# A gated feed-forward block on one core: the fourth of seven products for two tiles, and where lookup steps stand

## The chip, the cores and the metric

One core of one Trainium2 chip. The time is the device time of one execution in microseconds, the median over runs of the whole kernel. All matmuls are in float32.

## The reference

Eight sequences of 1024 rows and 512 columns. Each row is normalized; a small attention with decays gives `s`; a feed-forward block, whose three weight matrices are looked up in a table of 16 values, gives `g`; the result is `x + s * silu(g)`.

```python
def _ghost_linear(x, idx, lut):
    w = lut[idx]
    return jnp.einsum('bsh,oh->bso', x, w)
gate = _ghost_linear(x, gate_idx, lut)      # idx: 1376 x 512
up = _ghost_linear(x, up_idx, lut)          # idx: 1376 x 512
h = silu(gate) * up
g = silu(_ghost_linear(h, down_idx, lut))   # idx: 512 x 1376
x = x + s * g
```

## The kernel before

**Two phases.** Phase 1 (to about 584 us) goes over the eight sequences (batches) in chunks of 128 rows: normalization, transposition, projections, attention. In between, VectorE looks up the weights: `look_up` makes, for a piece of 128 x 1024 indices, three tests of a bit, a shift, eight leaves (L224) and seven predicated copies (L241), one instruction a step. GpSimd makes sums of the looked-up blocks, and DMAs write them to HBM: `quad_d` holds the weights of pairs of tiles with all seven combinations, `wgu_d` the plain seven products of a single tile. `phase_1` places the steps by hand: three places in each chunk, with so many steps in each (`steps`). DMAs that must wait are put off by a count of ticks (`defer`).

Phase 2 (from 584 us) takes the batches one by one. The 1376 hidden columns are eleven tiles of 128 (the last has 96). Gate and up are made together as one product of 2 x 2 blocks by a scheme with seven products instead of eight (`W_OF`, `X_OF` number them). For the quads of tiles (`quads`, two of four tiles each) each of these seven products is in turn made by seven smaller ones, in a `Node`: products 1, 5, 6, 2, 7, 3, 4 of 128 x 256, into four PSUM banks (s11, s12, s21, sE), with copies on ScalarE and additions on VectorE in PSUM between them. `Node.sixth` adds to bank s12 (L920), `Node.seventh` adds s21 into sE (L924), and product (2, 4), the fourth smaller product, accumulates into s21 after that. Two nodes are woven: while one is at its sixth and seventh, the first and fifth product of the following one are issued.

Tiles 8 and 9 are a pair. Their nodes serve two of the outer seven products each: (1, 6), (5, 7), (2, 3). The outer product 4 stands alone, and class `Fourth` makes it plainly: for each of the two tiles two matmuls of 128 x 512, as two banks' worth, from the plain weights in `wgu_d`. It fills the place of the following node after (2, 3).

The eleventh tile is made by `single`, with seven products of 96 x 512 (L845): before the quads for the first batch, after them for the seven others. Inside it `at_last(5)` lets VectorE make five sums of h for the down stage (L1122). Then `down` makes the third matrix's product from h, in nodes of its own kind (L1154, L1165).

In the first batch, the lookup of the last two rows of down weights (`left_weights`) still runs during the quads: `some(made, n)` makes n steps at each node.

`x` blocks in SBUF are overwritten with sums at one place each; `restore` fetches the plain block again by a DMA on ScalarE's queue, when the plain products need it. Weight tiles go through a ring of three slots (tag "wr"), loaded by SP's queue.

**Order.** `keep_order` fixes on every compute engine the order in which the code issues instructions. Each engine is in order, so an instruction that waits holds all behind it.

Of the kernel before, what the change touches and what calls it, by code (L numbers as in the profile page):

```python
# [9 lines left out]
F32 = mybir.dt.float32  # L10
# [4 lines left out]
ALU = mybir.AluOpType  # L15
AX = mybir.AxisListType

P = 128
# [30 lines left out]
def recurrent_block(ctx: ExitStack, tc, x, wq, wk, wv, wo, wg, decay_logits, out_scale, lut, gidx, uidx, didx, out):  # L49
# [196 lines left out]
    def ffn_weights(build, pool, pair_pool):  # L246
# [10 lines left out]
        def gate_up(o):  # L257
            s, m = OCH[o]
            n = 2 * NV * m
            idx = build.tile([P, NB], I32, name="idx", tag="idx", bufs=2)  # L260
            iv = idx[:, :n].rearrange("p (a b) -> p a b", b=m)
            gs, us = (src[:, s : s + m].rearrange("(c p) b -> p c b", p=P) for src in (gidx, uidx))
            nc.sync.dma_start(out=iv[:, 2:6, :], in_=gs)
            nc.sync.dma_start(out=iv[:, 0:2, :], in_=us[:, 0:2, :])
            nc.sync.dma_start(out=iv[:, 6:8, :], in_=us[:, 2:4, :])
            yield
            wf = pool.tile([P, 2 * NB], F32, name="wgu", tag="wgu", bufs=3)
            yield from look_up(build, wf[:, :n], idx[:, :n], P, n)
            w = wf[:, : 2 * n].rearrange("p (k two m) -> p k two m", two=2, m=m)
            a21, a11, a12, a22, s1, s2, s3, s4 = (w[:, k] for k in range(8))  # L270
            nc.gpsimd.tensor_tensor(s1, a21, a22, ALU.add)
            nc.gpsimd.tensor_tensor(s2, s1, a11, ALU.subtract)
            yield
            nc.gpsimd.tensor_tensor(s3, a11, a21, ALU.subtract)
            nc.gpsimd.tensor_tensor(s4, a12, s2, ALU.subtract)
            wide = wf[:, 2 * m : 2 * n].rearrange("p (a b) -> p a b", b=m)
            if o >= 4 * NQ:
                defer(3, lambda: nc.sync.dma_start(out=wgu_d[o], in_=wide))
            if o >= 2 * NK:
                return  # L280
            if o % 2 == 0:
                upper.append(w[:, 1:])
                return
            up, low = upper.pop(), w[:, 1:]
            to = quad_d[o // 4][:, :, o // 2 % 2, :].rearrange("p k (t m) -> p k t m", m=P)
            pair = pair_pool.tile([P, 7, 3, P], F32, name="pair", tag="pair")
            nc.sync.dma_start(out=to[:, :, 0:2, :], in_=up)
            b21, b22, b11, b12 = low[:, :, 0], low[:, :, 1], up[:, :, 0], up[:, :, 1]
            nc.gpsimd.tensor_tensor(pair[:, :, 0], b21, b22, ALU.add)
            yield  # L290
            nc.gpsimd.tensor_tensor(pair[:, :, 1], pair[:, :, 0], b11, ALU.subtract)
            yield
            if o >= 4 * NQ:
                for _ in range(4):
                    yield
            nc.gpsimd.tensor_tensor(b21, b11, b21, ALU.subtract)
            defer(3, lambda: nc.sync.dma_start(out=to[:, :, 2:4, :], in_=low))
            yield
            nc.gpsimd.tensor_tensor(pair[:, :, 2], b12, pair[:, :, 1], ALU.subtract)
            defer(4, lambda: nc.sync.dma_start(out=to[:, :, 4:7, :], in_=pair))  # L300
            for _ in range(3):
                yield
# [398 lines left out]
    def phase_1():  # L701
        nonlocal small, p_a, p_c, p_r
        with (
# [37 lines left out]
            for b in range(B + 1):  # L741
                following = project(b + 1, pools, sides, kept) if b + 1 < B else iter(())
                older = chunks(b - 1, (chk, blp), kept) if b else iter(())
                for k in range(NC):


                    if b == 0:
                        steps = (k > 0, k >= NC // 2, 2 * (k >= NC // 2))
                    elif b < B:
                        steps = ((1, 1, 4), (1, 2, 4), (1, 2, 4), (1, 2, 3))[k % 4]  # L750
                    else:
                        steps = (1, 0, 0)
                    tick()
# [40 lines left out]
    def phase_2():  # L794
        with (
# [32 lines left out]
                    nc.gpsimd.tensor_tensor(o, x1, x2, ALU.subtract)  # L828
                    yield

            def single(b, o, xs, h_tail, at_last, room):

                s, m = OCH[o]
                w = ring.tile([P, 14, P], F32, name=f"wr{b}_{o}", tag="wr")
# [8 lines left out]
                def product(ps, k, start, stop):  # L843
                    for n in range(2):
# [6 lines left out]
                            skip_group_check=True,  # L851
                        )

                product(pa, 1, True, False)
                nc.scalar.copy(u2, pa)
                product(pb, 6, True, True)
                nc.vector.tensor_tensor(u2, pb, u2, ALU.add)
                at_last(5)
                nc.scalar.copy(pc, u2)
                product(pe, 5, True, False)  # L860
                nc.scalar.copy(e, pe)
                product(pa, 2, False, True)
                nc.scalar.activation(sg, pa, AF.Silu)
                product(pc, 7, False, False)
# [9 lines left out]
            class Node:  # L874
# [2 lines left out]

                def __init__(self, b, q, ks, xs):  # L880
                    self.ks, self.xs = ks, xs

                    self.restores = ks if q == NQ else (4,) if (q, ks) == (NQ - 1, (4, 4)) else ()
                    name = f"{b}_{q}_{ks[0]}"
                    self.w = ring.tile([P, 2, 7, P], F32, name=f"wq{name}", tag="wr")
                    w = self.w.rearrange("p a t m -> p a (t m)")
# [2 lines left out]
                    else:  # L889
                        for a, k in enumerate(ks):  # L890
                            nc.sync.dma_start(out=w[:, a, :], in_=quad_d[q][:, W_OF[k], 0, :])
                    self.t = [bank(r, f"{r}{name}") for r in ("s11", "s12", "s21", "sE")]
                    self.name = f"e{name}"

                def product(self, n, i, start=False):
                    for a in range(2):
                        nc.tensor.matmul(  # L897
                            self.t[n][:, ts(a, H)],
                            lhsT=self.w[:, a, (0, 1, 6, 3, 4, 5, 2)[i - 1], :],
# [9 lines left out]

                def fifth(self):  # L910
                    self.product(3, 5, True)
                    self.e = tmp.tile([P, U], F32, name=self.name, tag="e")

                def fifth_copy(self):
                    nc.scalar.copy(self.e, self.t[3])  # L915
# [7 lines left out]
                    self.product(2, 7)  # L923
                    nc.vector.tensor_tensor(self.t[3], self.t[2], self.e, ALU.add)  # L924

            class Fourth:


                def __init__(self, b, xs, u3):
                    self.b, self.xs, self.u3 = b, xs, u3  # L930
                    self.w = ring.tile([P, 14, P], F32, name=f"w4{b}", tag="wr")
                    for r in range(2):
                        nc.sync.dma_start(
                            out=self.w[:, ts(r, 2), :], in_=wgu_d[4 * NQ + r][:, ts(W_OF[4], 2), :]
                        )

                def product(self, r, role):
                    ps = bank(role, f"{role}{self.b}_4_{r}")
                    for n in range(2):
                        nc.tensor.matmul(  # L940
                            ps,
                            lhsT=self.w[:, 2 * r + n, :],
                            rhs=self.xs[:, X_OF[4], ts(n, 2), :],
                            start=n == 0,
                            stop=n == 1,
                            skip_group_check=True,
                        )
                    o = self.u3[:, ts(r, 2), :]
                    return lambda: nc.vector.tensor_tensor(o, ps.rearrange("p (a t) -> p a t", a=2), o, ALU.add)

                def first(self):
                    self.product(0, "s11")()

                def fifth(self):
                    self.add = self.product(1, "sE")

                def fifth_copy(self):
                    self.add()

            def quads(b, xs, h, sums, made, at_last):  # L960

# [53 lines left out]
                def pair_steps():  # L1017
# [2 lines left out]
                        (t[:, :, :H], t[:, :, H:])  # L1020
                        for t in (tmp.tile([P, 4, U], F32, name=f"{k}{b}_l", tag=k) for k in ("p1", "u2"))
                    )
                    room[0] = u3

                    def of_h(half, n):
                        r, c = divmod(n, 2)
                        t = half * U + c * H
# [11 lines left out]
                    def node_23(t, n):  # L1039
# [2 lines left out]
                        nc.vector.tensor_tensor(of_h(1, n), t[n][:, H:], u2[:, n], ALU.add)  # L1042
                        nc.scalar.activation(of_h(1, n), of_h(1, n), AF.Silu)

                    def after_57():
                        for n in (0, 3, 1, 2):
                            nc.gpsimd.tensor_tensor(e5[:, n], e5[:, n], u3[:, n], ALU.add)

                    def after_23():
                        for half, other in ((0, u3), (1, e5)):  # L1050
                            for n in (0, 3, 1, 2):
                                nc.gpsimd.tensor_tensor(of_h(half, n), of_h(half, n), other[:, n], ALU.mult)

                    yield (1, 6), node_16, None
                    yield (5, 7), node_57, after_57
                    yield (2, 3), node_23, after_23

                room = [None]
                def every():
                    for q in range(NQ):  # L1060
                        for ks, empty, after in steps(q):
                            yield Node(b, q, ks, xs), empty, after
                    for ks, empty, after in pair_steps():
                        yield Node(b, NQ, ks, xs), empty, after
                    yield Fourth(b, xs, room[0]), None, None
                    yield None, None, None

                todo = every()
# [4 lines left out]
                while empty:  # L1073
# [7 lines left out]
                    at_last(node.ks == (2, 3))  # L1081
                    node.seventh()
                    empty(node.t, 3)
                    some(made, 4 if node.ks in ((1, 1), (5, 5)) else 1)
                    node.product(1, 3)
                    empty(node.t, 1)
                    at_last(node.ks in ((5, 7), (2, 3)))
                    if following:
                        following.fifth()
# [281 lines left out]
            for b in range(B):  # L1371
# [24 lines left out]
                    some(more, 2)  # L1396
                    single(b, NO - 1, xs, h_tail, sums_beside, tmp)
                made = left_weights(sp, wd_left) if b == 0 else iter(())
                quads(b, xs, h, more, made, no_sums if b else at_last)
                if b == 0:  # L1400
                    hold(out=wd_tail[: OCH[-1][1], :], in_=wdt_d)
                else:
                    single(b, NO - 1, xs, h_tail, at_last, tmp2)
                nodes_done = [0]

                def beside(k):
# [59 lines left out]
```

## Time and profile before

| | |
|---|---|
| median of 3 runs | 2103.63 us (2103.54 to 2104.08) |
| the profiled execution | 2103.83 us |
| its span, first to last instruction | 2101.9 us |
| mean granted TensorE clock | 0.999 |
| TensorE busy | 2086.2 us, 99% |
| VectorE busy | 1441.4 us, 69% |
| ScalarE busy | 943.6 us, 45% |
| GpSimd busy | 1038.5 us, 49% |
| DMA from HBM and to HBM | 281.95 MB, 75.63 MB |

PE is TensorE (PEld its weight loads), DVE VectorE, ACT ScalarE, POOL GpSimd, SP the queue that issues most DMAs. A float32 matmul stands in the trace as two records, each with its own weight load. Matmul records overlap: one of 256 columns lasts 380 ns and the next begins 216 ns after it. "idle before <- X" says how long an engine stood and what released it.

### The profile page before, as it was taken

The page shows a single profiled execution, that of the slowest core. Times are in us where ns is not written, and L with a number is a line of the kernel's source. Part 1 is how long each engine was busy: PE and PEld are TensorE (multiplying, and loading weights), DVE is VectorE, ACT ScalarE, POOL GpSimd, SP SyncE. Part 2 cuts the span into 40 slices and gives each one's busy share as a digit, 9 for nine tenths or more (in the row PEclk, how much of TensorE's full clock was granted, in tenths as well). Part 3 has the DMA queues.
Part 4 walks back from the last instruction along what each step waited for, and adds up shares of the span by engine and source line. Part 5 has one row for each costly group of instructions (what it writes and reads, how often), then busy time and mean ns, then how long its engine had stood idle before and what let it go on. Part 6 is the DMA issues. An engine that isn't in the chain of part 4 may idle for free.

```text
span 2101.9 us, 32181 instructions
## 1 busy us (share of the span) xinstructions
PE 2086.2 (99%) x11691; PEld 1751.8 (83%) x11691; DVE 1441.4 (69%) x2214; ACT 943.6 (45%) x2116; POOL 1038.5 (49%) x1050
## 2 busy tenths in 40 slices
PE   9999999999999999999999999999999999999999
PEld 7887888888878888797878888787988888797877
DVE  8889998879357775675567456656755665675567
ACT  4766676676344324423531542344144224424531
POOL 4554664364364456517443741664275265527432
PEclk9999999999999999999999999999999999999999
DMA  8766769654754734554454446345544634464442
GB/s 218 147 178 165 208 149 211 158 164 125 210 177 139 258 134 161 169 216 145 157 215 152 160 151 238 138 149 196 189 146 153 249 128 158 151 233 145 146 156 106
DMA packets 184347, 359.68 MB, mean 171 GB/s; under 512 B 50895, under 2 KB 122206, under 8 KB 184190
## 3 DMA queue, kind: packets, MB, share of 16 engines
q1 hardware_dynamic: 168742, 330.61, 50.4%
q10 hardware_dynamic: 10968, 12.34, 1.8%
q0 software_dynamic: 4480, 14.68, 1.7%
q8 instruction: 93, 1.52, 0.3%
q14 instruction: 64, 0.52, 0.1%
HBM read 281.95 MB, written 75.63 MB: 170 GB/s over the span
## 4 chain that ended last, share of the span: by engine, by line
PE 81%; DVE 2%; DMA 1%; issue 0%; POOL 0%; ACT 0%; SPq 0%; DVEq 0%; ACTq 0%
PE s L897 33%; PE sE L897 6%; PE s12d L1154 5%; PE s21d L1154 5%; PE s11d L1154 5%; PE fs L845 3%; PE pd L1272 3%; PE ps L1279 3%; PE pv L444 2%; PE sEd L1154 2%; PE po L684 2%; PE fsE L845 1%; PE s11d L1165 1%; PE s12d L1165 1%; PE s21d L1165 1%; PE sEd L1165 1%
## 5 line engine op out<-in xcount | busy, mean ns | idle before, releaser
L897 PE MATMUL s<-xs,wq 128*128 128x256 f32 x3264 | 732.3, 380 | 2.3 <-DVE s L920 2.3
L897 PEld LDWEIGHTS s<-xs,wq 128*128 128x128 f32 x3264 | 620.0, 190 | 98.8 <-issue 8.4
L920 DVE TENSOR_TENSOR s<-s,e 128x512 f32<-128x512 f32 x136 | 95.1, 699 | 189.4 <-ACT s L919 189.4
L1243 POOL TENSOR_TENSOR cu<-cu 128x256 f32<-128x256 f32 x32 | 35.1, 1096 | 306.5 <-DVE cl L1242 306.5
L444 PE MATMUL pv<-wvg_sb,xnT 128*128 128x387 f32 x512 | 177.5, 488 | 0.2 <-DMA wvg_sb<-in_wv 0.2
L828 POOL TENSOR_TENSOR xs<-xs 128x256 f32<-128x256 f32 x224 | 171.8, 793 | 6.8 <-PE fs L845 2.3
L924 DVE TENSOR_TENSOR sE<-s,e 128x512 f32<-128x512 f32 x136 | 95.1, 699 | 104.0 <-PE s L897 104.0
L990 POOL TENSOR_TENSOR u<-u,e 128x512 f32<-128x512 f32 x64 | 80.4, 1278 | 134.1 <-DVE u L986 101.9
L915 ACT COPY e<-sE 128x512 f32<-128x512 f32 x136 | 79.6, 585 | 142.5 <-PE sE L897 142.5
L897 PE MATMUL sE<-xs,wq 128*128 128x256 f32 x544 | 140.5, 381 | 0.0
L444 PEld LDWEIGHTS pv<-wvg_sb,xnT 128*128 128x128 f32 x512 | 94.2, 190 | 54.1 <-issue 0.4
L994 POOL TENSOR_TENSOR h<-h,u 128x512 f32<-128x512 f32 x64 | 81.1, 1287 | 110.2 <-DVE u L1001 110.2
L423 POOL TENSOR_SCALAR rstd<-rstd 128x1 f32<-128x1 f32 x56 | 26.6, 475 | 205.9 <-ACT junk L422 204.8
L908 ACT COPY s<-s 128x512 f32<-128x512 f32 x136 | 77.5, 570 | 109.6 <-PE s L897 106.2
L919 ACT COPY s<-s 128x512 f32<-128x512 f32 x136 | 77.5, 570 | 97.8 <-PE s L897 97.8
L1154 PE MATMUL s12d<-wdd,z 128*128 128x128 f32 x896 | 118.4, 275 | 0.6 <-ACT s12d L1176 0.6
L897 PEld LDWEIGHTS sE<-xs,wq 128*128 128x128 f32 x544 | 104.0, 191 | 14.3
L1154 PEld LDWEIGHTS s12d<-wdd,z 128*128 128x128 f32 x896 | 109.0, 192 | 0.8 <-ACT s12d L1176 0.8
L224 DVE TENSOR_SCALAR leaf<-idx,lut_x,lut_sb 128x1024 int32<-128x1024 int32 (+2 forms) x119 | 108.2, 933 | 0.0
L641 POOL TENSOR_TENSOR qb<-ga,q_tab 128x384 f32<-128x384 f32 x56 | 77.1, 1377 | 55.5 <-DVE ga L637 37.8
L241 DVE COPY_PREDICATED leaf<-bit,leaf 128x1024 f32<-128x1024 uint8 (+2 forms) x68 | 93.0, 1368 | 1.7
L1283 POOL TENSOR_TENSOR gx<-gx,cu 128x512 f32<-128x512 f32 x32 | 40.8, 1278 | 82.0 <-DVE cu L1281 64.5
(266 smaller groups left out, 4517.3 us busy)
## 6 DMA issues: line engine op xcount, KB each, us to landing
wq<-quadd SPq DMA_DIRECT2D x112, 896.0 KB, 4.5
wdd<-wdd SPq DMA_DIRECT2D x56, 896.0 KB, 4.7
xs<-xsd SPq DMA_DIRECT2D x56, 512.0 KB, 6.5
wq<-quadd SPq DMA_DIRECT2D x48, 448.0 KB, 4.0
x<-in_x SPq DMA_DIRECT2D x64, 256.0 KB, 6.4
xsd<-ts SPq DMA_DIRECT2D x16, 1024.0 KB, 12.8
gx<-in_x SPq DMA_DIRECT2D x64, 256.0 KB, 6.1
out<-gx POOLq DMA_DIRECT2D x56, 256.0 KB, 2.3
```

The costliest lines, as they stand in the source:

```text
L224: nc.vector.tensor_scalar(o.bitcast(I32), iv, lut_x[:rows, k, :], lut_i[:rows, k, 0:1], ALU.bitwise_and, ALU.bitwise_xor,)
L241: nc.vector.copy_predicated(o, bits[level - 1][:rows, :n], t[:rows, :n])
L444: nc.tensor.matmul(pv, lhsT=xnT[:, v, ts(c, P)], rhs=wvg_sb[:, v, :], start=(v == 0), stop=(v == NV - 1))
L828: nc.gpsimd.tensor_tensor(o, x1, x2, ALU.subtract)
L845: nc.tensor.matmul(ps, lhsT=w[:, 2 * W_OF[k] + n, :m], rhs=xs[:, X_OF[k], 2 * n : 2 * n + 2, :], start=start and n == 0, stop=stop and n == 1,
L897: nc.tensor.matmul(self.t[n][:, ts(a, H)], lhsT=self.w[:, a, (0, 1, 6, 3, 4, 5, 2)[i - 1], :], rhs=self.xs[:, X_OF[self.ks[a]], D_OF[i], : ...
L920: nc.vector.tensor_tensor(self.t[1], self.t[1], self.e, ALU.add)
L924: nc.vector.tensor_tensor(self.t[3], self.t[2], self.e, ALU.add)
L990: nc.gpsimd.tensor_tensor(o[:, n], o[:, n], other[:, n], ALU.add)
L994: nc.gpsimd.tensor_tensor(of_h(half, n), of_h(half, n), two(other[:, n]), ALU.mult)
L1154: nc.tensor.matmul(self.t[n][:, ts(a, P)], lhsT=self.lhs[i][:, e, ts(a, P)], rhs=self.w[:, e, D_OF[i], :], start=start and a == 0 and e == ...
L1165: nc.tensor.matmul(self.t[n][:, ts(a, P)], lhsT=self.left[:, ts(2 * (n // 2) + a, P)], rhs=wd_left[:, D_OF[self.k], ts(n % 2, P)], start=F ...
```

## The change

1. In phase 1, the third place of chunks 0 and 4 of a batch makes three lookup steps instead of four.
2. The plain weights of tiles 8 and 9 are no longer written to `wgu_d`, and four empty steps that kept the pair's sums apart from that write are gone.
3. In the first batch's quads, the steps of `left_weights` at the nodes (1, 1) and (5, 5) are not four in a row but two before product (1, 3) and one or two after it.
4. `Fourth` is gone. The outer product 4 of tiles 8 and 9 is a `Node` with one entry, `(4,)`: seven products of 128 x 256, with its weights from `quad_d`. In the first batch it is the last node of the quads. In the others it is kept in `last`, and `beside_single` issues its parts between the eleventh tile's products: first and fifth before product 1; sixth and (0, 2) before 6; seventh and (1, 3) before 5; (2, 4) before 2.
5. The restore of the x block of product 4 moves from the last quad's last node to this node, and the multiplies of h by u3 wait for it.

```diff
-            if o >= 4 * NQ:
+            if o >= 2 * NK:
                 defer(3, lambda: nc.sync.dma_start(out=wgu_d[o], in_=wide))
...
-            if o >= 4 * NQ:
-                for _ in range(4):
-                    yield
...
-                        steps = ((1, 1, 4), (1, 2, 4), (1, 2, 4), (1, 2, 3))[k % 4]
+                        steps = ((1, 1, 3), (1, 2, 4), (1, 2, 4), (1, 2, 3))[k % 4]
...
+            def beside_single(node, empty, after, restore):
+                node.first()
+                node.fifth()
+                node.fifth_copy()
+                yield
+                node.sixth()
+                node.product(0, 2)
+                empty(node.t, 0)
+                yield
+                node.seventh()
+                restore(*node.restores)
+                empty(node.t, 3)
+                node.product(1, 3)
+                empty(node.t, 1)
+                yield
+                node.product(2, 4)
+                empty(node.t, 2)
+                after()
+                yield
...
+                next(beside, None)
                 product(pa, 1, True, False)
                 nc.scalar.copy(u2, pa)
+                next(beside, None)
                 product(pb, 6, True, True)
                 nc.vector.tensor_tensor(u2, pb, u2, ALU.add)
                 at_last(5)
                 nc.scalar.copy(pc, u2)
+                next(beside, None)
                 product(pe, 5, True, False)
                 nc.scalar.copy(e, pe)
+                next(beside, None)
                 product(pa, 2, False, True)
...
-            class Fourth:
...
-                    yield Fourth(b, xs, room[0]), None, None
...
+                    yield (4,), node_4l, lambda: multiply_by(0, u3)
...
+                        if ks == (4,) and b > 0:
+                            last.append((Node(b, NQ, ks, xs), empty, after, restore))
+                        else:
+                            yield Node(b, NQ, ks, xs), empty, after
...
-                    some(made, 4 if node.ks in ((1, 1), (5, 5)) else 1)
+                    some(made, 2 if node.ks in ((1, 1), (5, 5)) else 1)
                     node.product(1, 3)
                     empty(node.t, 1)
+                    some(made, (node.ks == (1, 1)) + 2 * (node.ks == (5, 5)))
...
-                    single(b, NO - 1, xs, h_tail, at_last, tmp2)
+                    single(b, NO - 1, xs, h_tail, at_last, tmp2, beside_single(*last[0]))
```

More of the change, by code (lines that the diff above doesn't have):

```diff
@@ L829, in sums_of_x, with single @@
                     yield
-            def single(b, o, xs, h_tail, at_last, room):
+            def beside_single(node, empty, after, restore):
[17 more added lines that the diff above has]
+                yield
+            def single(b, o, xs, h_tail, at_last, room, beside=iter(())):
                 s, m = OCH[o]
@@ L881, in __init__ @@
                     self.ks, self.xs = ks, xs
-                    self.restores = ks if q == NQ else (4,) if (q, ks) == (NQ - 1, (4, 4)) else ()
+                    self.restores = ks if q == NQ else ()
                     name = f"{b}_{q}_{ks[0]}"
@@ L891, in __init__ @@
                             nc.sync.dma_start(out=w[:, a, :], in_=quad_d[q][:, W_OF[k], 0, :])
-                    self.t = [bank(r, f"{r}{name}") for r in ("s11", "s12", "s21", "sE")]
+                    self.n = len(ks) * H
+                    self.t = [bank(r, f"{r}{name}")[:, : self.n] for r in ("s11", "s12", "s21", "sE")]
                     self.name = f"e{name}"
                 def product(self, n, i, start=False):
-                    for a in range(2):
+                    for a in range(len(self.ks)):
                         nc.tensor.matmul(
@@ L911, in fifth @@
                     self.product(3, 5, True)
-                    self.e = tmp.tile([P, U], F32, name=self.name, tag="e")
+                    self.e = tmp.tile([P, U], F32, name=self.name, tag="e")[:, : self.n]
                 def fifth_copy(self):
@@ L924, in seventh, with quads @@
                     nc.vector.tensor_tensor(self.t[3], self.t[2], self.e, ALU.add)
-            class Fourth:
[L929 to L960, printed above, removed]
+            def quads(b, xs, h, sums, made, at_last, last):
                 def restore(*ks):
@@ L1022, in pair_steps @@
                     )
-                    room[0] = u3
                     def of_h(half, n):
@@ L1043, in node_23, with multiply_by @@
                         nc.scalar.activation(of_h(1, n), of_h(1, n), AF.Silu)
+                    def multiply_by(half, other):
+                        for n in (0, 3, 1, 2):
+                            nc.gpsimd.tensor_tensor(of_h(half, n), of_h(half, n), other[:, n], ALU.mult)
                     def after_57():
@@ L1049, in after_23, with node_4l @@
                     def after_23():
-                        for half, other in ((0, u3), (1, e5)):
-                            for n in (0, 3, 1, 2):
-                                nc.gpsimd.tensor_tensor(of_h(half, n), of_h(half, n), other[:, n], ALU.mult)
+                        multiply_by(1, e5)
+                    def node_4l(t, n):
+                        nc.vector.tensor_tensor(u3[:, n], t[n], u3[:, n], ALU.add)
                     yield (1, 6), node_16, None
@@ L1056, in pair_steps @@
                     yield (2, 3), node_23, after_23
-                room = [None]
+                    yield (4,), node_4l, lambda: multiply_by(0, u3)
                 def every():
@@ L1063, in every @@
                     for ks, empty, after in pair_steps():
-                        yield Node(b, NQ, ks, xs), empty, after
-                    yield Fourth(b, xs, room[0]), None, None
+                        if ks == (4,) and b > 0:
+                            last.append((Node(b, NQ, ks, xs), empty, after, restore))
+                        else:
+                            yield Node(b, NQ, ks, xs), empty, after
                     yield None, None, None
@@ L1398, in phase_2 @@
                 made = left_weights(sp, wd_left) if b == 0 else iter(())
-                quads(b, xs, h, more, made, no_sums if b else at_last)
+                last = []
+                quads(b, xs, h, more, made, no_sums if b else at_last, last)
                 if b == 0:
```

## The prediction

> **What bounds the kernel now.** I read the granted clock first (0.999 over the span), then the page's engine table and chain, then the chain in order of time, then TensorE's own waits, then the timeline at the places that the change touches.
>
> ```profile
> PE 2086.2 (99%) x11691; PEld 1751.8 (83%) x11691; DVE 1441.4 (69%) x2214; ACT 943.6 (45%) x2116; POOL 1038.5 (49%) x1050
> ```
>
> TensorE is busy 99% of the span and the chain that ended last is 81% PE: what any other engine does costs nothing until TensorE waits for it. In the chain by time a node of 28 matmul records (seven products of four) follows the one before at 6.04 us (846.13, 852.18, 858.22) and one batch the one before at 188.29 us (968.73, 1157.02, 1345.31), with no wait in it. So a change is worth the TensorE records that it removes, less every new wait. TensorE's waits are few:
>
> ```profile
> PE po L684 <- DVE pr L662: 2.5, 3, 1.4
> PE s L897 <- DVE s L920: 2.3, 1, 2.3
> PE pe L505 <- DVE ts L515: 1.6, 3, 0.8
> ```
>
> The columns are total us, times, longest. The middle one lies in the first batch's nodes, where phase 2 still does a lookup:
>
> ```profile
> 644.88 3.07 DVE L224 TENSOR_SCALAR leaf<-idx,lut_x,lut_sb 128x1024 int32<-128x1024 int32 x2
> ...
> 647.99 2.26 DVE L241 COPY_PREDICATED leaf<-bit,leaf 128x1024 f32<-128x1024 uint8 x1
> ...
> 650.15 1.74 DVE L224 TENSOR_SCALAR leaf<-idx,lut_x,lut_sb 128x1024 int32<-128x1024 int32 x1
> 651.81 0.69 DVE L920 TENSOR_TENSOR s<-s,e 128x512 f32<-128x512 f32 x1
> ```
>
> Four lookup steps in a row hold back VectorE's L920, TensorE stands from 650.28 to 652.55, and then the clock halves for one window (columns: window, its length, busy us and counts, clock, DMA):
>
> ```profile
> 649.52:652.93 3.41, 1.14 (x6) 0.69 (x5) 3.41 (x4) 0.56 (x1) 1.82 (x1) 1.00 0.31 128
> 652.93:656.34 3.41, 3.41 (x10) 2.70 (x9) 2.77 (x5) 0.25 (x1) 0.00 (x0) 0.50 0.02 5
> ```
>
> Node to node the two nodes here take 9.15 (644.94 to 654.09) and 7.16 us (to 661.25) instead of 6.04: 4.2 us lost, 2.4 of it the wait (counted to where the record before stops streaming) and 1.8 the half clock.
>
> **Matmuls** (lines are those of before). `Fourth` is eight records of 512 columns, at 0.429 us each (28 of L845 take 884.80 to 896.82): 3.43 us. The seven products are 14 records of 256 columns, at 0.216 (24 take 5.18): 3.02. That is -0.41 us a batch, -3.3 in eight.
>
> **Seven batches (b > 0), first new wait.** Node (2, 3) now runs with no following node woven in. By the timeline at b = 1 its products would end: sixth 877.92, product (0, 2) 878.78, seventh 879.65, (1, 3) 880.51. Its ScalarE copy L919 ends at 878.74, just in time for the seventh. VectorE runs L920 to 879.47, then two narrow adds (0.33 us apart, from 879.38), then L924, which reads the bank that product (2, 4) writes: 880.05 to 880.74. So (2, 4) starts at 880.79: +0.27 us. `Fourth`'s 1.72 us between had hidden this.
>
> **Second new wait, the large one.** In the changed program's order VectorE has, inside the eleventh tile: the add of product 6 (L857's), five sums for the down stage (L1122, from `at_last(5)`), and only then the new node's L924-type add, which reads the bank s21 that product (2, 4) of the same node accumulates into. That product stands between the eleventh tile's products 5 and 2, and TensorE is in order, so all behind it waits. By the steps of 0.216 and 0.429 a record: (2, 4) of node (2, 3) ends 881.65, the new first and fifth 882.51, product 1 884.23, the new sixth and (0, 2) 885.09, product 6 886.81, the new seventh and (1, 3) 887.67, product 5 889.39: TensorE is there. VectorE's add of product 6 starts 0.25 us after that product, at 887.06, the sums 0.61 later, at 887.67. They take, by the timeline of before:
>
> ```profile
> 888.49 0.69 DVE L857 TENSOR_TENSOR t<-fs,t 96x512 f32<-96x512 f32 x1 [2.73 <-PE fs L845]
> 889.10 0.68 DVE L1122 TENSOR_TENSOR z<-h 128x512 f32<-128x512 f32 x1
> 889.81 1.10 DVE L1122 TENSOR_TENSOR z<-z,h 128x512 f32<-128x512 f32 x1
> 890.84 0.68 DVE L1122 TENSOR_TENSOR z<-h 128x512 f32<-128x512 f32 x1
> 891.44 0.68 DVE L1122 TENSOR_TENSOR z<-h,z 128x512 f32<-128x512 f32 x1
> 892.04 1.21 DVE L1122 TENSOR_TENSOR sx<-h 128x1024 f32<-128x1024 f32 x1
> ```
>
> Start to start 0.71, 0.61 (the 1.10 is beside a busy GpSimd; here GpSimd waits for the new node's adds), 0.60, 0.60, then 1.13 for the wide one: 3.65 us, so the new add runs 891.32 to 891.75 (0.43, L1188's row) and TensorE goes on at 891.80: +2.4 us. In before the same five sums hid because product 4, the next to need VectorE, came two products later. Bounds: 1.8, if all five follow each other at the shortest step, 0.60; 4.7, if GpSimd stretches all as it stretched that one (1.10 for 0.68). I take 2.4, because nothing of GpSimd's is due then.
>
> Per batch -0.41 + 0.27 + 2.4 = +2.3; seven, +15.8. Behind this product TensorE is the bound again; ScalarE's and VectorE's ends move along.
>
> **Transfers.** The eleventh tile's weights (L835) still go at 877.25, once node (5, 7) frees their ring slot, and land 5.0 us later (median): 882.25, while product 1 now wants them at 882.51 instead of 884.80. I count nothing and bound it by 0.3 a batch. The new node's weights are one issue on SP's queue instead of two (448 KB for 256), 10 us ahead. The restore of its x slot (128 KB, 2.0 us) moves into ScalarE's queue behind the copy L859, near 888.4; it lands near 890.4, and product 4 wants it after 897. Without that cover it would cost up to its 2.0.
>
> **The clock.** After the 2.3 us gap above, the window that held it had 1.14 us of matmul in 3.41 and the next was granted 0.50. The 1.37 us gap at 98 us, inside one window, cost nothing. A gap of 2.3 us lies inside one window, or mostly, in about half of the batches, so I take half: 7 x 0.5 x 1.8 = +6.3; bounds 0 and 12.6. The Trainium skill (TensorE: Matmul & The Clock Gate, The HAM clock gate) has the clock fall after an idle window of about 3.4 us, and speaks of gaps above that; by that rule alone no gap here would cost clock, and the sum would be 6.3 lower. The row above disagrees, with a shorter gap, and I go by it.
>
> **First batch.** The lookup steps go 2 + 1 and 2 + 2 around product (1, 3), 12 a round for 13. By counting them on, the four of 644.88 become a copy and two leaves, before the same L920. Beside GpSimd, at 2.26, 1.53 and 1.5, they end near 650.3; TensorE, ready at 650.1, goes on near 651.05. So 0.9 of the 4.2 stays: -3.3 (bounds -4.2 and -1.9). The next batch of four is two leaves and two copies (4.4 us beside an idle GpSimd), inside the node's slack of 4.6.
>
> Here the eleventh tile went first, so the new node stands alone at the end, with nothing between its products. Its copy t2 waits on ScalarE behind the last Silu of node (2, 3), which waits for VectorE's adds and sums there: about 707.6 by 700.96 + one add of 0.7, three sums (0.7, 0.7, 1.3) and nine narrower ops, while TensorE is there at 705.7. Then (1, 3) waits some 0.45 for the add behind those sums, (2, 4) some 0.3 for the next, and (2, 4) of node (2, 3) 0.3 as in the other batches: 0.3 + 1.9 + 0.45 + 0.3 - 0.41 for the matmuls = +2.5. Bounds: 1.1 (VectorE without the sum of 1.3) and 4.6 (with the clock halved and 0.3 more). The multiplies for h that the down stage's first `rest` reads come early enough: the first of them is free at about 709.6, `rest` comes 4.5 after 709.7.
>
> **Phase 1.** In seven batches the third place of chunks 0 and 4 makes 3 lookup steps instead of 4, so 14 come later; four empty steps and two writes of 896 KB go. The lookups still end about one chunk later than before, well ahead of the end of phase 1, where VectorE is less full (133.95 of 200 us in 400 to 600, 178.93 in the first 200). TensorE's waits there sum to some 5 us, so it cannot gain more; a bunching of steps behind `pr` or `ts` could lose as much as the four steps above, 4. I take 0.
>
> **Sum:** 15.8 + 6.3 - 3.3 + 2.5 = +21.3 on the profiled execution's 2103.83 us (span 2101.9 and 1.93 around it; the median of runs is 2103.63, 0.2 lower): 2125.
>
> **Rivals.**
> - The new waits cost no clock: 2103.8 + 15.0 = 2119. For it: the 1.37 us gap that cost none. Chance 0.25.
> - The clock halves in all seven batches: 2131. For it: the one gap of this length did. Chance 0.22.
> - The new node is covered, and the kernel ends no slower: VectorE would have to reach the node's add by 889.4, so the five sums would have to take 1.25 us instead of 3.65; from there on only the matmuls count (seven times -0.41, -2.9) and the first batch (-3.3 + 2.5): 2100, or 2098.7 with the lone node at its lower bound. The rows of the sums speak against it. Chance 0.06, half of it within 0.2%.
> - Phase 1's new order adds 4 us or more: 2129 to 2135. Chance 0.07.
> - My forecast, some of the gaps at half clock: 0.40.
>
> **Range.** 2112 (1.8 a wait, no clock loss, phase 1 gains 2) to 2141 (every clock lost, a third of the GpSimd stretching, phase 1 loses 4). Outside lies the covered case and some of the tails. A measurement of this kernel tells about 0.2%, 4.2 us, from no change. Faster 0.03, same 0.03, slower 0.94.
>
> **What would show it.** Right: a TensorE wait for the new node's VectorE add, seven times, about 2.3 us each; batch period near 190.6 or 192.4 us in place of 188.29; several half-clock windows; the wait at 650 under 1 us. Wrong: TensorE at 99.5% with a period of 187.9, or the eleventh tile's products waiting for a DMA.

## The result, and the profile after

The changed kernel takes 2122.2 us (median of 4 runs, 2121.65 to 2123.05) beside 2103.59 for the kernel before: a measured ratio of 1.0093, 95% interval 1.0078 to 1.0108 (1.0088 by the two medians). It is 0.9% slower. The profiled execution has a span of 2120.7 us against 2101.9.

The engine table of the page, kernel after:

```profile
PE 2090.1 (99%) x11739; PEld 1760.3 (83%) x11739; DVE 1453.2 (69%) x2246; ACT 950.2 (45%) x2140; POOL 1028.9 (49%) x1050
```

TensorE's busy time rose by 3.9 us, though by the prediction's count its matmuls need 3.3 less: a record that no neighbour overlaps counts to its full length, and one at half clock lasts longer (512 columns 1.06 us, against 0.59). The rest of the 18.8 is idle time. TensorE's own waits, kernel after (total us, times, longest):

```profile
PE s L921 <- DVE sE L948: 15.8, 8, 2.2
PE po L681 <- DVE pr L659: 1.8, 3, 1.1
PE pe L502 <- DVE ts L512: 1.5, 2, 0.8
PE s L921 <- ACT s L943: 1.4, 1, 1.4
PE psc L657 <- DVE ga L634: 1.4, 1, 1.4
```

The first line is new: product (2, 4) of the new node waits for the add of `seventh` (now L948) in all seven later batches; the eighth, of 0.35, is node (2, 3) of the first. VectorE's timeline at b = 1, kernel after:

```profile
886.51 0.69 DVE L877 TENSOR_TENSOR t<-fs,t 96x512 f32<-96x512 f32 x1 [0.88 <-PE fs L863]
887.12 0.68 DVE L1119 TENSOR_TENSOR z<-h 128x512 f32<-128x512 f32 x1
...
889.65 1.22 DVE L1119 TENSOR_TENSOR sx<-h 128x1024 f32<-128x1024 f32 x1
890.78 0.43 DVE L948 TENSOR_TENSOR sE<-s,e 128x256 f32<-128x256 f32 x1
```

and TensorE's there:

```profile
887.17 1.88 PE L863 MATMUL fsE<-xs,wr 128*96 128x512 f32 x4
891.26 0.70 PE L921 MATMUL s<-xs,wq 128*128 128x256 f32 x2 [2.21 <-DVE sE L948]
```

The five sums fill 887.12 to 890.78, 3.66 us. The last record of product 5 lasts 0.59 us, of which it streams 0.43, so TensorE stands 0.16 us longer than the row says: 2.37 us. Two small waits before it hide in the overlap of records: the 26 records up to and with the new node's first product (875.59 to 881.58) take 5.99 us instead of 5.61. In the chain by time the first full node of each of the seven later batches starts thus, kernel after (the lines between are left out):

```profile
779.84 4.40 PE s L921 x20
970.58 4.40 PE s L921 x20
1161.75 4.40 PE s L921 x20
1352.51 4.40 PE s L921 x20
1543.26 4.40 PE s L921 x20
1735.69 4.40 PE s L921 x20
1926.43 4.40 PE s L921 x20
```

A batch takes 190.74 us instead of 188.29, the second 191.17, the fifth 192.43. The second waited for the eleventh tile's weights (DMA wr, 0.43 in all), the fifth ran one window at half clock (columns: window, length, busy us and count of PE, PEld, DVE, ACT and POOL, granted clock, DMA share, GB/s; the fourth batch first, then the fifth):

```profile
1460.26:1463.67 3.41, 1.47 (x4) 0.33 (x2) 3.38 (x6) 0.82 (x2) 0.00 (x0) 1.00 0.18 56
1463.67:1467.08 3.41, 3.14 (x9) 1.46 (x10) 1.40 (x4) 0.59 (x1) 2.10 (x3) 1.00 0.44 101
1651.40:1654.82 3.42, 1.21 (x4) 0.30 (x3) 3.32 (x6) 0.58 (x1) 0.00 (x0) 1.00 0.15 45
1654.82:1658.23 3.41, 3.41 (x6) 1.47 (x7) 1.09 (x3) 0.00 (x0) 2.08 (x3) 0.50 0.42 97
```

The waits in the fourth and fifth batch are equally long; only in the fifth does the whole gap lie inside one window.

In the first batch the lookup's wait fell from 2.27 to 0.60 with no half clock behind it, and at the end TensorE waits three times, first in node (2, 3), then twice in the lone node, and the clock halves behind it (TensorE's timeline, kernel after; the first line is the lookup's wait):

```profile
650.51 1.13 PE L921 MATMUL s<-xs,wq 128*128 128x256 f32 x4 [0.60 <-DVE s L944]
...
700.34 1.99 PE L921 MATMUL s<-xs,wq 128*128 128x256 f32 x8 [0.35 <-DVE sE L948]
703.78 0.70 PE L921 MATMUL s<-xs,wq 128*128 128x256 f32 x2 [1.44 <-ACT s L943]
705.09 1.76 PE L921 MATMUL s<-xs,wq 128*128 128x256 f32 x4 [0.61 <-DVE s L944]
706.64 1.92 PE L1151 MATMUL s11d<-wdd,h 128*128 128x128 f32 x8
```

### The profile page after: what moved, and what is told of

Read it like the earlier page. It is cut to its first block, busy times and chain, and to the rows that moved or that the text cites. A ratio compares the mean times of both kernels' runs of the same rounds, so it can differ in the third digit from the quotient of the medians.

```text
span 2120.7 us, 32343 instructions
## 1 busy us (share of the span) xinstructions
PE 2090.1 (99%) x11739; PEld 1760.3 (83%) x11739; DVE 1453.2 (69%) x2246; ACT 950.2 (45%) x2140; POOL 1028.9 (49%) x1050
## 4 chain that ended last, share of the span: by engine, by line
PE 91%; DVE 5%; DMA 2%; issue 1%; ACT 0%; POOL 0%; SPq 0%; DVEq 0%; ACTq 0%; POOLq 0%
PE s L921 34%; PE pv L441 7%; PE sE L921 6%; PE s11d L1151 5%; PE s12d L1151 5%; PE s21d L1151 5%; PE fs L863 3%; PE po L681 3%; PE pd L1269 3%; PE ps L1276 3%; PE sEd L1151 2%; PE pe L502 2%; PE pc L502 2%; PE pa L502 2%; PE psc L657 2%; PE pu L667 1%
## 5 line engine op out<-in xcount | busy, mean ns | idle before, releaser
L921 PE MATMUL s<-xs,wq 128*128 128x256 f32 x3360 | 758.3, 380 | 18.5 <-DVE sE L948 15.8
L921 PEld LDWEIGHTS s<-xs,wq 128*128 128x128 f32 x3360 | 635.8, 190 | 127.6 <-DVE sE L948 25.4
L948 DVE TENSOR_TENSOR sE<-s,e 128x512 f32<-128x512 f32 x144 | 98.5, 684 | 103.3 <-PE s L921 103.3
L932 ACT COPY s<-s 128x512 f32<-128x512 f32 x144 | 80.6, 559 | 109.5 <-PE s L921 107.5
L943 ACT COPY s<-s 128x512 f32<-128x512 f32 x144 | 80.6, 560 | 97.5 <-PE s L921 97.5
L985 POOL TENSOR_TENSOR h<-h,e 128x512 f32<-128x512 f32 x64 | 81.2, 1304 | 0.0
## 6 DMA issues: line engine op xcount, KB each, us to landing
xsd<-ts SPq DMA_DIRECT2D x16, 1024.0 KB, 14.1
```

The costliest lines, as they stand in the source:

```text
L921: nc.tensor.matmul(self.t[n][:, ts(a, H)], lhsT=self.w[:, a, (0, 1, 6, 3, 4, 5, 2)[i - 1], :], rhs=self.xs[:, X_OF[self.ks[a]], D_OF[i], : ...
L985: nc.gpsimd.tensor_tensor(of_h(half, n), of_h(half, n), two(other[:, n]), ALU.mult)
```

## Experiments

The theory was that VectorE's order makes the wait (the sums ahead of the node's add), against the rival that VectorE, or something beside it, has too much to do there.

**The sums after the node's part.** In `single` of the changed kernel:

```diff
-                at_last(5)
                 nc.scalar.copy(pc, u2)
                 next(beside, None)
+                at_last(5)
```

> The changed kernel with the five sums of at_last(5) issued after the third part of the new node instead of before it; the work is the same, only VectorE's order differs. Theory (order): the wait of 2.37 us before product (2, 4), with the 0.1 that the restart costs, goes in all seven batches; a batch falls from 190.74 to about 188.3 us, the one half-clock window among them goes too, and the time is about 2103 us. Rival (VectorE has too much to do in this stage, wherever it stands): the wait moves to the next product that needs VectorE, product 4 of the eleventh tile, and a batch stays at 190 us or more, 2118 us or more.

Measured: 2103.96 us beside 2103.38 of before (ratio 1.0002, interval 0.9993 to 1.0012). Batches take 188.27, two of them 188.61 and 188.67. VectorE's timeline of this run shows the same work in another order, and in the later batches TensorE no longer waits for it:

```profile
887.00 0.69 DVE L877 TENSOR_TENSOR t<-fs,t 96x512 f32<-96x512 f32 x1 [0.89 <-PE fs L863]
887.61 0.42 DVE L948 TENSOR_TENSOR sE<-s,e 128x256 f32<-128x256 f32 x1
...
892.17 1.21 DVE L1119 TENSOR_TENSOR sx<-h 128x1024 f32<-128x1024 f32 x1
893.31 0.41 DVE L1046 TENSOR_TENSOR u_l<-s,u_l 128x256 f32<-128x256 f32 x1
```

It is the order. One line moved gives back nearly the whole loss.

**Six sums, and three.** The changed kernel with `at_last(6)` and nothing later, then with `at_last(3)` and three later.

> The changed kernel with six sums instead of five at that place (the sixth, 128x1024, taken from later in the tile). Theory: the wait grows by one step of the wide sum, 1.13 us, to 3.5 us in each of seven batches, a batch is 191.9 us without clock loss; 2.2 us of idle in one window of 3.41 us halved the clock, 1.94 did not, so with 3.3 idle most of the batches, some 5 of 7, lose another 1.7: 2122 + 7.9 + 6.8 = 2137 us. If the clock fell only after a whole window of 3.4 us idle, no batch would lose it: 2128 us. Rival (VectorE's total, not its order): a batch is unchanged, 190.7.

> The changed kernel with three sums at that place instead of five, and the other two with the one later in the tile. Theory: two steps of 0.60 and 1.13 us less in front of the new node's add, so the wait falls from 2.21 to about 0.48, a batch takes 189.0 us, no batch's clock falls; about 2108 us. Rival (the wait is not the sums'): unchanged, 190.7 a batch.

Measured with six, one run: 2142.6 us (2137 forecast), all seven waits 3.34 us. The one batch without clock loss takes 191.87, as forecast; the others 193.57 to 194.74. With three, one run: 2109.32 us (2108 forecast), waits of 0.47 us, batches of 189.30, one of 189.78, and no half clock. So the wait is the sums' time less what TensorE has beside them, step by step. The clock is dearer than forecast: in six batches of seven it halved, in four of them for two windows. In these four the rest of the gap fell into the first half-clock window; in the other two that window was full. Windows of the run with six, batches 2 and 4:

```profile
1081.18:1084.59 3.41, 1.26 (x3) 0.16 (x1) 3.38 (x6) 0.61 (x2) 0.00 (x0) 1.00 0.18 56
1084.59:1088.01 3.42, 2.23 (x4) 1.35 (x5) 2.32 (x5) 0.00 (x0) 1.67 (x3) 0.50 0.02 4
1088.01:1091.42 3.41, 3.41 (x5) 1.13 (x4) 0.00 (x0) 0.59 (x1) 0.42 (x1) 0.50 0.79 265
...
1470.30:1473.71 3.41, 1.40 (x4) 0.28 (x2) 3.38 (x6) 0.75 (x2) 0.00 (x0) 1.00 0.16 48
1473.71:1477.12 3.41, 2.08 (x6) 1.11 (x7) 2.46 (x5) 0.00 (x0) 1.53 (x3) 1.00 0.23 34
```

**The split lookup steps alone**, in the kernel before:

```diff
-                    some(made, 4 if node.ks in ((1, 1), (5, 5)) else 1)
+                    some(made, 2 if node.ks in ((1, 1), (5, 5)) else 1)
                     node.product(1, 3)
                     empty(node.t, 1)
+                    some(made, (node.ks == (1, 1)) + 2 * (node.ks == (5, 5)))
```

> The kernel before, with only the lookup steps of phase 2 set in twos around product (1, 3). Theory: the wait of 2.27 us near 650 us shrinks to 0.6 and the half clock behind it does not come; batches stay at 188.29; 2103.6 - 3.4 = about 2100.2 us. Rival (the wait comes from GpSimd's multiplies slowing VectorE, whatever the order): 2103.6, the wait unchanged.

Measured: 2100.96 us, ratio 0.999 (0.9981 to 1.0, so only just clear of no change). The wait is 0.96 us, with no half clock, batches 188.29; from the eleventh tile's first product to the second batch 191.16 us instead of 194.18, so 3.0 of the 3.4 forecast. By the trace this part of the change is worth having. VectorE's steps are still longer beside GpSimd's multiplies (a predicated copy of 128x1024 takes 2.38 us beside them and 1.31 after them), and the wait is not gone.

**The node between (5, 7) and (2, 3)**, in all batches, nothing woven into the eleventh tile:

```diff
                     yield (5, 7), node_57, after_57
+                    yield (4,), node_4l, None
                     yield (2, 3), node_23, after_23
-                    yield (4,), node_4l, lambda: multiply_by(0, u3)
```

> The changed kernel with the node of the outer product 4 woven between the nodes (5, 7) and (2, 3) in all batches, and nothing between the eleventh tile's products. Theory: no 2.4 us wait; node (2, 3) is still without a following node, so its two short waits of 0.37 us in sum stay: -0.41 + 0.37 a batch, 188.25 us; the first batch saves 3.4 at the lookup and loses about 1 at its end instead of 3.1: about 2100.5 us. Rival (the sums u3 from GpSimd come too late for this node, and VectorE waits for them with the node's other adds behind): 0.5 to 1 us more in each batch, 2104 to 2108 us.

Measured: 2106.93 us, ratio 1.0018 (1.0008 to 1.0028). Batches take 188.64 to 189.65, not the 188.25 forecast, and the cause is neither the theory's nor the rival's. TensorE's waits, this run:

```profile
PE fs L863 <- DMA xs<-xsd: 3.0, 6, 1.2
```

The restore of the x blocks of products 2 and 3 is issued at 882.92 on ScalarE's queue, and product 2 of the eleventh tile, due at 887.55, starts at 888.87. With the new node out of the way it comes earlier than the block lands. The first batch did profit: 191.72.

**Phase 1's steps alone**, in the kernel before, `(1, 1, 4)` to `(1, 1, 3)`:

> The kernel before with only phase 1's third place at three lookup steps instead of four in chunks 0 and 4. Theory (phase 1 moves nothing that TensorE waits for): phase 2's first matmul of the eleventh tile at 584 to 585 us, where three profiles with the steps of before have it at 584.0 to 585.2, and no difference that the interval can tell, 2103. Rival (the lookups ran too close to their limit, or now bunch later): 2 us or more either way.

Measured: 2109.35 us, ratio 1.0033 (1.0021 to 1.0045): the rival was right. Its TensorE has a wait that before did not have, of 5.8 us at 570 us, and two windows at half clock behind it (the kernel after has that line with 1.4, above):

```profile
PE psc L660 <- DVE ga L637: 5.8, 1, 5.8
```

SP's queue tells why (the start of each issue; this run first, then before):

```profile
555.77 0.51 SPq L343 DMA_DIRECT2D wdd<-pair  x1
556.37 0.61 SPq L468 DMA_DIRECT2D gTd<-g  x1
...
570.53 0.33 SPq L483 DMA_DIRECT2D ga<-gTd  x1
```

```profile
540.37 2.27 SPq L343 DMA_DIRECT2D wdd<-pair  x1
...
553.72 0.36 SPq L468 DMA_DIRECT2D gTd<-g  x1
...
565.05 0.33 SPq L483 DMA_DIRECT2D ga<-gTd  x1
```

The last write of down weights goes at 555.77 now, and the write of the gates, which stands behind it, directly after, at 556.37, though VectorE has the gates ready at 553.16; in before it went at 553.72. The read that must follow its landing goes at 570.53, in before at 565.05, and VectorE's product with the gates, `ga`, waits for that. Of these 5.5 us the later issue of the write is 2.65; the rest is that the write takes 14.1 us to land instead of 11.3, and why it does is not shown. In the changed kernel the last write of down weights goes at 551.09 and the read at 566.34: with four empty steps dropped, the lookups are four steps further on. The two edits belong together; that these four steps, and not the two missing writes, make up for the loss is argued from the code and was not tried alone.

**Versions without these waits.** Sums after the node's part; the node's first and fifth product woven into (2, 3) in the later batches; in the first batch the node between:

> The changed kernel with the sums after the third part, the new node's first and fifth product woven into node (2, 3) in the seven later batches, and in the first batch the new node between (5, 7) and (2, 3). Theory: no wait is left in a batch, so it takes the -0.41 us of the matmuls whole: 187.88 us; the first batch 191.7 from the start of the eleventh tile, as in the run with the node between, against 194.2 before; 2103.6 - 2.9 - 2.5 = about 2098.2 us. Rival (a batch cannot go under 188.29, because something beside TensorE paces it, the weights' loads or VectorE): 2101 us.

Measured: 2102.52 us, ratio 0.9993 (0.9984 to 1.0001), not told from before, and 4.3 us over the forecast. First batch 191.74 as forecast, batches 187.88 to 188.51, most of them over the 187.88 that the matmuls alone would take. That makes 1.3 us in six batches; the rest stays open, for the profiled execution, 2100.26, was the fastest of eleven. Next, with the plain product in the first batch and phase 1 as before:

> As the woven run, but with the plain fourth product of before in the first batch, and phase 1 as before. Theory: batches 187.88; the first batch 191.2, as in the run with the split steps alone; about 2097.7 us. Rival (the new order in phase 1 is worth more than that): over 2099.

Measured: 2100.59 us, ratio 0.9984 (0.9975 to 0.9993), first batch 191.19, batches 187.93 to 188.35. The time is over the rival's 2099, but phase 1 is not behind it: the first full node starts at 598.01 here and at 598.50 in the woven run. What is left over 187.88, 0.05 to 0.5 us, is the eleventh tile's first product waiting for its weights' landing, now wanted sooner:

> As the run with the plain product in the first batch, with the eleventh tile's weights loaded by two DMAs, the 96 KB of product 1 ahead of the rest. Theory (product 1 waits for the landing of all 672 KB, some 0.2 us a batch): the wait goes, batches 187.88 in all seven, 1.7 us less than that run, about 2099 us beside its 2100.6. Rival (the landing is late because other transfers run then, whatever its size): batches stay at 187.9 to 188.35 and the time at 2100.6.

```diff
-                nc.sync.dma_start(out=w[:, :, :m], in_=wgu_d[o])
+                for part in (slice(0, 2), slice(2, 14)):
+                    nc.sync.dma_start(out=w[:, part, :m], in_=wgu_d[o][:, part, :])
```

Measured: 2097.55 us, ratio 0.9975 (0.9965 to 0.9984), and from batch to batch the chain by time has the 187.88 that the matmuls alone give, so the wait was for the whole of that load, as the theory had it (four lines of the chain):

```profile
777.28 4.40 PE s L922 x20
965.16 4.40 PE s L922 x20
1153.04 4.40 PE s L922 x20
1340.91 4.40 PE s L922 x20
```

## Why the prediction was right, and where it was off

Forecast 2125, measured 2122.2. The mechanism was right: the wait, its place and what releases it. By the forecast's own steps, on the spans (+18.8 us):

| step | forecast | measured |
|---|---|---|
| seven batches, matmuls and both waits | +15.8 (2.3 each) | +17.2 (2.45 each) |
| eleventh tile's weights | 0, at most 0.3 a batch | +0.4, one batch |
| clock in seven batches | +6.3 | +1.7, one batch |
| first batch, lookup | -3.3 | -3.4 |
| first batch, lone node | +2.5 | +3.1 |
| phase 1 | 0 | -0.4 |

That the total came within 3 us is partly luck: the clock was put 4.6 us too high, the waits, the weights and the lone node together 2.4 too low, and 2122.2 lies midway between the forecast and the rival without clock loss, 2119.

**The waits** were right in place and size: the sums took 3.66 us for the 3.65 worked out, the add began at 890.78 for the 891.32 given, in a batch that began 0.60 us earlier, and the run with the sums moved shows that this is the cause. The 0.2 that each batch lost beyond the forecast comes from the restart cost told below, three times 0.10, less 0.1 by which the waits themselves were shorter; the small waits before the large one came to 0.37 with it, not 0.27.

**The clock** is the term that was mis-sized. I took half of the batches; one of seven lost its clock in the profiled execution. Measured, the rule is sharper than the row I had. In phase 2 of five profiles (before, after, sums after, six sums, three sums), the full-clock windows of 3.41 us in which TensorE streamed for up to 1.19 us (0.216 us for each record of 256 columns, 0.429 for one of 512) were all followed by half clock; those with 1.31 or more were not; of two between, in the run with six sums, 1.26 was and 1.23 was not. (The busy times in the rows above are larger, for they count each record to its end: the two windows with the gaps of the fourth and fifth batch streamed 1.31 and 1.04, those of the run with six sums 1.10 and 1.23.) So some 2.2 us of a gap of 2.37 must lie in one window. 190.74 us is 55.88 windows, so from batch to batch the gap starts 0.4 us earlier in its window. By the trace it starts 2.07, 2.10, 1.72, 1.31, 0.91, 2.19 and 1.79 us behind the window's start in the seven batches (the second kept its place, for that batch lost 0.43 us to its weights). The fifth is the first that lies whole in its window, and its half clock put the next one 1.28 us later again. By these steps, an estimate, about one batch in four halves its clock and not one in two; that it was one of seven depends on where in its window the first gap fell.

The Trainium skill (TensorE: Matmul & The Clock Gate, The HAM clock gate) asks for an idle window. The measurements decide against it: gaps of 2.4 and 3.5 us halved the clock here, with no window wholly idle.

**The lone node** cost 0.6 more than forecast, within its bounds: its waits came at the places named, the copy's shorter (1.44 for 1.9), and the clock halved there, which I had only in the upper bound. That this cost no more is luck again: two waits that before has at the start of the first batch's down stage, and that the forecast did not look at, are gone (before):

```profile
PE s12d L1154 <- ACT s12d L1176: 0.6, 1, 0.6
PE s11d L1165 <- DVE sx L1122: 0.4, 1, 0.4
```

With the overlap and the restart they are 1.5 us, about what the half clock cost.

**Phase 1** came out as forecast by luck. I looked at VectorE's load and TensorE's wait totals; what counted was SP's queue, in which the lookups' DMAs move against the others. One of its edits alone costs 6.4 us, and the others nearly cancel it. The -0.4 cannot be told from nothing: in four profiles with phase 1 as before the first full node starts between 598.01 and 599.17, in the kernel after at 597.99.

## What to carry to other kernels

When a new dependent step is woven between others, write down, for each engine, what stands ahead of its link in that engine's order: work that was harmless filler becomes part of the chain, here five sums worth 2.4 us in each of seven batches, and moving one line repairs it. In these runs a gap cost more than its length once it left TensorE streaming for less than about 1.2 of a clock window's 3.41 us. Steps that carry DMAs move a queue's order with them; follow the queue's next reader, not only the engine that made the step.

## What the runs showed of the hardware

- In front of a product of 256 columns, each wait of TensorE on another engine costs about 0.10 us after it ends: the first record after the wait at 891.26 is followed 0.320 us later instead of 0.216, so its pair lasts 0.70 us, where a pair that did not wait lasts 0.59. The same stands behind the wait on the copy L943 at 878.19. With three such waits a batch it is 2.2 us in seven batches.
- Behind waits of 3.34 us the half clock lasted for two windows, 6.83 us, in four of six cases, and a batch lost up to 2.9 us to it (194.74 against 191.87), not the 1.7 of one window.
